# An edge-gated graph layer: PSUM banks of z and of the w_v products filled by VectorE or ScalarE ahead of the matmuls, in fixed banks

## The chip, the cores and the metric

The kernel runs on one core of one Trainium2 chip. The metric is the device time of one execution in microseconds. Times of the kernel before are the median of three runs; the profile is one more execution, taken by the hardware profiler.

## The reference, cut to what matters

There are 16 batches, 1024 nodes, 256 features, and a sparse 1024 x 1024 adjacency `adj` that every batch shares. For each batch:

```python
pre_u = h @ W1[:256];  pre_v = h @ W1[256:]
hidden = relu(pre_u[:, :, None] + pre_v[:, None] + b1)      # per edge u, v
S      = sigmoid(hidden @ W2 + b2)
a_t    = einsum('uv,ud->vd', S * adj, h)
m_t    = einsum('uv,ud->vd', adj, h) * h
z      = beta1*h + beta2*(a_t @ Wa + ba) + beta3*(m_t @ Wm + bm)
```

The change touches how b1 enters `pre_v`, and how `beta1*h` and the biases enter `z`.

## The kernel before, in words

**Blocks and steps.** The output is made in 32 blocks: 4 groups of 4 batches times 8 tiles of 128 target nodes. A block has 10 steps (two windows of 64 targets, five columns of 128 edges each), so there are 320 steps, counted n; k is the block and s the step in it. Groups 0 and 1 come first, interleaved, then group 2 (blocks 16 to 23) and group 3 (24 to 31).

**One step.** POOL gathers, for 128 edges, the rows of their source nodes out of a table in DRAM (`fetch`, L515): the first half of a row holds h times w_u for 4 batches, the second half h itself. TensorE spreads the target's w_v products over the edges with a 0/1 matrix (`expand`, L610, tile `pc`, two buffers). VectorE adds `pc` to the fetched row (`add`, L646, the operation at L648), then takes relu times W2 and its sum once per batch (`gate`, L650, four operations at L656). ScalarE makes the sigmoid (L659) and scales four pieces of the left matrix with it (L661); `left_adj` (L619, L625) prepares the left matrix of the entry after. TensorE then sums the edges into `acc` (`aggregate`, L664, L673), with entries n-3 and n-2 taken at odd steps n.

**Once per half window.** ScalarE copies `acc` to `ev` (`half_end`, L678), TensorE transposes it and ScalarE copies the result into `LT` (`turn_over`, L683, L691 and L694), and VectorE multiplies one half by h (L705).

**Once per block.** `halves` (L473) makes the w_v products of the next block in two parts of two batches: a PSUM bank gets b1 from a matmul of `unit` by a row pair `b1_p` (`add_row`, L448), eight matmul records (L445) add the product, and ScalarE copies the bank twice, to `X` (L482) and `low` (L483); VectorE takes the difference (L484), and ScalarE makes three casts of it, each at a step of its own (L486, L489). `rows` (L452) makes w_u products for the table of a later group and stores them. `block_end` (L710) makes z of the block before, again in two parts: bias row by `add_row`, w_a matmuls in one step, w_m matmuls in the next (L722), ScalarE copies the bank into `LT`'s space (L736), VectorE forms beta1 h + z (L737) a step later, and SP sends the result out (L739). In group 3 the second part adds beta1 h by identity matmuls instead (L726), and ScalarE writes the result (L728).

**PSUM.** `pc` takes four banks (two buffers of two), `acc0` and `acc1` one each, and a pool `psm` of two buffers serves all else in turn (`small`, L220): transposes, w_u, w_v and z products, list products.

**What sets the order.** All five engines run in the order of the program (`manual_schedule`, L492). In the main loop (L882) step n of the program holds, for n below LAST = 230: aggregation and `ev` copies, mark cast (when s is 1 or 6), `expand(n + 2)`, `products(n, k, s)` (L821), `add(n + 1)`, `gate(n)`, `left_adj(n + 1)`, then what is due (`do(n)`, L904). From LAST on, `expand(n + 2)` and `products` stand after `gate`, `left_adj` and `do`. In `products`, z of the block before stands at s = 4, 5, 6, 7, the parts of `halves` at s = 1, 3, 4, 6, 7 (from step 10 on) and transposes at s = 8, 9, 0, 2. `plan` (L787) gives the steps of the loads of hT and of the w_u parts. For the first 110 steps, `lists` (L242) builds the edge lists of later tiles in pieces between VectorE's other work (`fill`, L640).

Of the kernel before, what the change touches and what calls it, by code (L numbers as in the profile page):

```python
# [13 lines left out]
P = 128  # L14
# [3 lines left out]
def kernel(  # L18
# [46 lines left out]
    GB = 4  # L65
# [116 lines left out]
    unit = fixed([P, P], "unit", FR)  # L182
    nc.vector.tensor_scalar(unit, upto[:, :P], 0.0, None, ALU.is_ge)
# [34 lines left out]
    psm = main.enter_context(tc.tile_pool(name="psm", bufs=2, space=bass.MemoryType.PSUM))  # L218

    def small(name):  # L220
        return psm.tile([P, 512], FP, name="misc")
# [20 lines left out]
    def lists(vt):  # L242
# [35 lines left out]
        used = lst.tile([P, S], FP, name="used", bufs=4)  # L278
# [9 lines left out]
        for i in range(4):  # L288
            nc.tensor.matmul(pw[:, i:i + 1], sums[:, i].rearrange("p w q v -> p (w q v)"), R[:, 0:1],
                             start=True, stop=True)  # L290
        yield "wait"
        first = R[:, 1:2]
        from_ = lst.tile([P, 1], FP, name="from", bufs=4)
# [23 lines left out]
        none = lst.tile([P, 1], FP, name="none", bufs=4)  # L317
# [6 lines left out]
        last = lst.tile([P, 1], FP, name="last", bufs=4)  # L324
# [4 lines left out]
        RR = lst.tile([P, NW, RC], FP, name="RR", bufs=2)  # L329
        few = lst.tile([P, E], mybir.dt.uint8, name="few", bufs=2)  # L330
# [13 lines left out]
        L = lst.tile([P, M, RC], FP, name="L", bufs=2)  # L344
# [103 lines left out]
    def add_row(p, parts):  # L448
        nc.tensor.matmul(p, unit, parts.unsqueeze(1).to_broadcast([P, 2, D]),  # L449
                         start=True, stop=False, skip_group_check=True)  # L450
# [22 lines left out]
    def halves(k):  # L473
        X = cuts[k] = big.tile([P, NW, GD], FR, name="X")
        low = one.tile([P, GD], FP, name="low")
        for h in range(2):
            step = yield
            c = slice(2 * h * D, (2 * h + 2) * D)
            p = small("p")
            add_row(p, b1_p)  # L480
            half_product(p, hTs[order[k]], w_v, h, True)
            nc.scalar.copy(X[:, 0, c], p)  # L482
            nc.scalar.copy(low[:, c], p)  # L483
        after(step + (2 if k else 1), lambda: nc.vector.tensor_tensor(low, low, X[:, 0, :].bitcast(FP), ALU.subtract))  # L484
        yield
        nc.scalar.copy(X[W:, 1, :], X[W:, 0, :].bitcast(FP))  # L486
        for w in range(NW):
            yield
            nc.scalar.copy(X[(1 - w) * W:(2 - w) * W, w, :], low[w * W:(w + 1) * W])  # L489
# [16 lines left out]
    T = TW * NW  # L506

    BS = NG * NT
# [28 lines left out]
    b1_b = load_rows(b1, D, "b1_b", nc.sync, spare[:, 0])  # L537
# [92 lines left out]
    be1_eye = []  # L630
# [79 lines left out]
    def block_end(k):  # L710
# [3 lines left out]
        for h in range(2):  # L714
            for i, wt in ((1, w_a), (0, w_m)):
                step = yield
                if i:
                    pz = small("pz")
                    add_row(pz, bias_p)
# [4 lines left out]
            if h == 1 and g == NG - 1:  # L724
                for bb in range(2):
                    nc.tensor.matmul(pz[:, bb * D:(bb + 1) * D], be1_eye[0], hb[h][:, bb, :], start=False, stop=True,  # L726
                                     skip_group_check=True)
                nc.scalar.copy(hb[h], pz.rearrange("p (b d) -> p b d", b=2))  # L728
                b = g * GB + 2 * h
                after(step + 2, lambda hb=hb[h], b=b: nc.sync.dma_start(  # L730
                    out[b:b + 2, vt * P:(vt + 1) * P, :].rearrange("b p d -> p b d"), hb))
                continue
            z = pz.rearrange("p (b d) -> p b d", b=2)
            if step >= ROOM:
                z = LTs[k][:, 2 * h].rearrange("p k c n -> p (k c n)").rearrange("p (b d) -> p b d", b=2)
                nc.scalar.copy(z, pz.rearrange("p (b d) -> p b d", b=2))  # L736
            after(step + 1, lambda hb=hb[h], z=z: nc.vector.scalar_tensor_tensor(hb, hb, be1, z, ALU.mult, ALU.add))  # L737
            b = g * GB + 2 * h
            after(step + 2, lambda hb=hb[h], b=b: nc.sync.dma_start(  # L739
# [53 lines left out]
    plan(turn[NT:], ((1, 2, 4), (2, 8, 9), (5, 12, 18), (10, 19, 22), (20, 28, 29), (23, 32, 38), (30, 39, 42), (40, 48, 49)))  # L793
    for g, first in ((2, 60), (3, 140)):
        plan([(g, vt) for vt in range(NT)], ((first - 4 + 10 * i, first + 8 + 10 * i, first + 12 + 10 * i)
# [25 lines left out]
    def products(n, k, s):  # L821
# [4 lines left out]
        z = 3 if n < ROOM else 4  # L826
        if z <= s < z + 4 and 0 < k < BS:
            if s == z:
                end = block_end(k - 1)
                next(end)  # L830
            go(end, n)
        if ROOM <= n < total - T:
# [18 lines left out]
        later = n >= ROOM  # L851
        if k + 1 < BS and s - later in (0, 2, 3, 5, 6):
            if s == later:
                parts = halves(k + 1)
                next(parts)
            go(parts, n)

# [4 lines left out]
    ROOM, MORE, LISTS = 10, 3, 110  # L862
    LAST = (BS - NT - 1) * T
# [18 lines left out]
    for n in range(total + 2):  # L882
        k, s = divmod(n, T)
# [9 lines left out]
        if n < LAST:  # L893
# [3 lines left out]
            products(n, k, s)  # L897
        if n + 1 < total:
# [10 lines left out]
        if n == 1:  # L909
            bias = load_rows(bm, D, "bias", nc.sync, spare[:, 1])  # L910
# [24 lines left out]
        if n >= LAST:  # L935
            products(n, k, s)
        if n == LISTS:
# [4 lines left out]
            be1_eye.append(more.tile([P, P], FP, name="be1_eye"))  # L942
            nc.vector.tensor_scalar(be1_eye[0], ident, be1, None, ALU.mult)
# [118 lines left out]
```

## Time and profile before

| what | value |
| --- | --- |
| time, median of 3 runs | 1072.59 us (1072.10 to 1073.26) |
| the profiled execution | 1082.24 us |
| its span, mean granted TensorE clock | 1080.4 us, 0.99 |
| DMA | 394.56 MB, mean 365 GB/s |
| chain that ended last, by engine | PE 40%, DVE 34%, issue 10%, ACT 8%, DMA 5% |
| L656, VectorE relu times W2 | 1280 times, mean 419 ns |
| L648, VectorE addition of pc | 320 times, mean 1212 ns |
| L737, VectorE beta1 h + z | 55 times, mean 744 ns |
| L449, TensorE b1 rows and bias rows | 64 and 62 times, mean 411 and 397 ns |
| L726, TensorE identity matmuls | 28 times, mean 379 ns |

PE is TensorE's matmuls, PEld its weight loads, DVE is VectorE, ACT is ScalarE, POOL is GpSimd, SP the engine that issues most transfers. Matmuls overlap in the record, and so do operations of VectorE and ScalarE with the one after: what an operation costs its queue is read as the distance from its start to the next start, which is shorter than its mean.

### The profile page before, as it was taken

How to read it: one execution, taken by the hardware profiler on the slowest of the kernel's cores; microseconds unless marked ns; L12 is line 12 of the kernel's file. 1: busy time of each engine (PE TensorE's matmuls, PEld its weight loads, DVE VectorE, ACT ScalarE, POOL GpSimd, SP SyncE). 2: the span in 40 equal slices, each digit the busy share in tenths (PEclk: the TensorE clock that was granted, in tenths of full speed). 3: DMA queues.
4: the chain of work that ended last, by engine and by line, in shares of the span. 5: the costliest groups of instructions: out<-in, count | busy, mean ns of one | idle time of the engine just before them, and what ended most of it. 6: DMA issues, size and time to landing. Idle time of an engine off the chain costs nothing.

```text
span 1080.4 us, 24120 instructions
## 1 busy us (share of the span) xinstructions
PE 1020.1 (94%) x7673; PEld 731.3 (68%) x7673; DVE 1017.6 (94%) x3481; ACT 862.6 (80%) x2616; POOL 459.3 (43%) x456
## 2 busy tenths in 40 slices
PE   7777999999999999999999999999999999999996
PEld 6654676776666776677777767777766667666654
DVE  8687999998999999999999999999999999999993
ACT  3246787788888887898888888889889889999983
POOL 2666676555257334553333334333333333333330
PEclk9989999999999999999999999999999999999999
DMA  9999899999999999999999999999999999999991
GB/s 283 327 340 385 313 339 381 362 382 378 403 352 371 408 381 385 379 403 395 404 393 399 412 384 392 408 396 389 381 361 370 369 348 368 365 381 369 365 341 44
DMA packets 147752, 394.56 MB, mean 365 GB/s; under 512 B 18224, under 2 KB 94512, under 8 KB 111408
## 3 DMA queue, kind: packets, MB, share of 16 engines
q0 software_dynamic: 50544, 301.16, 70.9%
q1 hardware_dynamic: 83776, 78.66, 22.9%
q10 hardware_dynamic: 13296, 13.11, 3.5%
q8 instruction: 63, 1.03, 0.4%
q14 instruction: 73, 0.60, 0.1%
HBM read 396.93 MB, written 50.33 MB: 414 GB/s over the span
## 4 chain that ended last, share of the span: by engine, by line
PE 40%; DVE 34%; issue 10%; ACT 8%; DMA 5%; POOL 2%; another core or an unknown queue 0%; POOLq 0%; DVEq 0%; ACTq 0%
DVE fetched L656 16%; DVE fetched L648 12%; PE acc L673 10%; PE misc L722 10%; PE misc L445 9%; PE pc L615 7%; DMA fetched<-table,uidx 3%; PE misc L691 2%; ACT left L661 2%; DVE LT L705 1%; ACT X L489 1%; PE misc L449 1%; DVE low L484 1%; DVE h_blk L737 1%; DMA hT__635<-in_xT_dram 1%
## 5 line engine op out<-in xcount | busy, mean ns | idle before, releaser
L518 POOL DMA_INDIRECT fetched<-table,uidx x320 | 339.4, 1061 | 529.0 <-PE acc L673 389.0
L656 DVE SCALAR_TENSOR_TENSOR fetched<-fetched,w_b 128x256 f32<-128x256 f32 x1280 | 478.0, 419 | 0.0
L648 DVE TENSOR_TENSOR fetched<-fetched,pc 128x1024 f32<-128x1024 f32 x320 | 387.7, 1212 | 29.9 <-PE pc L615 19.4
L661 ACT ACTIVATE left<-left,gt 128x32 f32<-128x32 f32 (+1 forms) x1280 | 299.6, 305 | 10.4
L673 PE MATMUL acc<-fetched,left 128*32 128x256 f32 x4096 | 273.4, 385 | 6.3 <-ACT gt L659 3.7
L615 PE MATMUL pc<-X,mark 128*128 128x512 f32 x640 | 243.7, 462 | 10.9 <-DVE fetched L648 9.3
L673 PEld LDWEIGHTS acc<-fetched,left 128*32 128x32 f32 x4096 | 127.6, 109 | 112.1 <-issue 29.1
L615 PEld LDWEIGHTS pc<-X,mark 128*128 128x128 f32 x640 | 105.4, 189 | 88.9 <-issue 41.6
L659 ACT ACTIVATE gt<-sc,b_b 128x4 f32<-128x4 f32 x320 | 95.9, 300 | 46.7 <-DVE fetched L656 37.5
L722 PE MATMUL misc<-w_m,LT 128*128 128x256 f32 x496 | 117.3, 379 | 0.0
L722 PE MATMUL misc<-w_a,LT 128*128 128x256 f32 x496 | 117.2, 379 | 0.0
L445 PE MATMUL misc<-w_v,hT 128*128 128x256 f32 x448 | 107.6, 383 | 0.0
L722 PEld LDWEIGHTS misc<-w_a,LT 128*128 128x128 f32 x496 | 93.8, 189 | 15.3 <-issue 0.4
L722 PEld LDWEIGHTS misc<-w_m,LT 128*128 128x128 f32 x496 | 93.8, 190 | 15.1
L625 ACT ACTIVATE left<-onehot,val 128x64 f32<-128x64 bf16 (+1 forms) x320 | 102.9, 322 | 0.0
L385 POOL DMA_INDIRECT val<-in_adjT_dram,vidx x80 | 87.2, 1090 | 34.4 <-issue 20.4
L656 DVE DVE_READ_ACCUMULATOR fetched<-fetched,w_b 128x1 f32 x1280 | 100.7, 79 | 0.0
L691 PE MATMUL misc<-ident,ev 128*128 128x128 f32 x512 | 79.5, 278 | 18.5 <-issue 7.0
L445 PEld LDWEIGHTS misc<-w_v,hT 128*128 128x128 f32 x448 | 86.4, 193 | 14.3
L691 PEld LDWEIGHTS misc<-ident,ev 128*128 128x128 f32 x512 | 60.7, 141 | 45.7 <-ACT ev L681 15.2
L482 ACT CAST X<-misc 128x512 fp32r<-128x512 f32 x64 | 37.1, 580 | 55.2 <-PE misc L445 48.0
L445 PE MATMUL misc<-w_u,hT 128*128 128x256 f32 x320 | 76.6, 386 | 4.0 <-issue 3.8
(185 smaller groups left out, 1011.3 us busy)
## 6 DMA issues: line engine op xcount, KB each, us to landing
h_blk<-table SPq DMA_DIRECT2D x62, 256.0 KB
out_dram<-h_blk SPq DMA_DIRECT2D x62, 256.0 KB
hT<-in_xT_dram SPq DMA_DIRECT2D x28, 512.0 KB
table<-in_x_dram ACTq DMA_DIRECT2D x24, 512.0 KB
table<-tab SPq DMA_DIRECT2D x48, 256.0 KB
fetched<-table,uidx POOLq DMA_INDIRECT x320
table<-in_x_dram SPq DMA_DIRECT2D x8, 512.0 KB
table<-fetched SPq DMA_DIRECT2D x8, 512.0 KB
```

The costliest lines, as they stand in the source:

```text
L385: nc.gpsimd.indirect_dma_start(out=val[:, i, j:j + 1], out_offset=None, in_=adj_flat, in_offset=bass.IndirectOffsetOnAxis(ap=vidx[:, i, j: ...
L445: nc.tensor.matmul(p[:, bb * D:(bb + 1) * D], hT[:, 2 * h + bb, i, :], wt[:, i, :], start=(i == 0 and not begun), stop=(i == DC - 1), skip ...
L518: nc.gpsimd.indirect_dma_start(out=fetched[at_slot[n]], out_offset=None, in_=table[g], in_offset=bass.IndirectOffsetOnAxis(ap=uidx[:, vt * ...
L615: nc.tensor.matmul(pcs[n][:, c], marks[n // TW][:, j * P:(j + 1) * P], cuts[k][:, w, c], start=True, stop=True)
L625: nc.scalar.activation(lefts[n][:, :m, 1::GB, :], onehot[:, i, o:o + m, :].unsqueeze(2).to_broadcast([P, m, GB // 2, V]), AF.Copy, scale=v ...
L648: nc.vector.tensor_tensor(t, t, pcs.pop(n), ALU.add)
L656: nc.vector.scalar_tensor_tensor(t[:, b, :], t[:, b, :], 0.0, w2_b, ALU.max, ALU.mult, accum_out=sc[:, b:b + 1])
L659: nc.scalar.activation(gt, sc, AF.Sigmoid, bias=b2_b)
L661: nc.scalar.activation(lefts[n][:, :m, 2 * b, :], lefts[n][:, :m, 1 + b // 2 * GB, :], AF.Copy, scale=gt[:, b:b + 1])
L673: nc.tensor.matmul(accs[h][b * 2 * V:(b + 1) * 2 * V, r, :], left[:, i, 2 * b - b % 2:2 * b - b % 2 + 2].rearrange("p k v -> p (k v)"), f[ ...
L691: nc.tensor.transpose(pt[:, r, :, c, :], ev[:, r, c * P:(c + 1) * P], ident)
L722: nc.tensor.matmul(pz[:, bb * D:(bb + 1) * D], LTs[k][:, 2 * h + bb, i if bb else 1 - i, c, :], wt[:, c, :], start=False, stop=(i == 0 and ...
```

## The change

Bank 1 of `psm` becomes the bank of z and of the w_v products, bank 0 that of everything else (from step 10 to three steps before the end). The additive part is written into bank 1 ahead of the matmuls, which then all add. `seed_x` copies b1 into it by ScalarE (steps 11 to 221, at s = 9 and s = 1). `seed_z` writes beta1 h + bias by VectorE before step 230, or beta1 h by ScalarE from then on, where the bias row stays as an adding matmul; it stands at s = 3 and s = 6 (s = 5 for the last block). The identity matmuls, the VectorE operation after z and the copy into `LT` are gone; ScalarE copies z's bank to `h_blk`, and the transfer out follows a step later. The w_v parts stand a step sooner, the second part of z a step later, the w_u parts at other steps.

```diff
+    unit_ = fixed([P, 1], "unit", FR)
+    nc.vector.tensor_scalar(unit_, row, 0.0, None, ALU.is_ge)
+    unit = unit_.to_broadcast([P, P])
...
-    psm = main.enter_context(tc.tile_pool(name="psm", bufs=2, space=bass.MemoryType.PSUM))
-    def small(name):
-        return psm.tile([P, 512], FP, name="misc")
+    psm = main.enter_context(tc.tile_pool(name="psm", bufs=1, space=bass.MemoryType.PSUM))
+    def small(name, bank=None):
+        if bank is None and ROOM <= now[0] < BS * T - 3:
+            bank = 0
+        elif bank is None:
+            bank = turn_of[0] % 2
+            turn_of[0] += 1
+        return psm.tile([P, 512], FP, name=f"misc{bank}")
...
+        if vt >= EARLY - 1:
+            held_pw = lst.tile([P, 4], FP, name="pws", bufs=2)
+            nc.scalar.copy(held_pw, pw[:, :4])
+            pw = held_pw
...
+    def seed_x():
+        p = small("p", 1)
+        nc.scalar.copy(p.rearrange("p (b d) -> p b d", d=D), b1_b.unsqueeze(1).to_broadcast([P, 2, D]))
+        seeds.append((p, False))
+
+    def seed_z(k, h, step):
+        p = small("pz", 1)
+        out_ = p.rearrange("p (b d) -> p b d", d=D)
+        if step < LAST:
+            nc.vector.scalar_tensor_tensor(out_, hbs[k][h], be1, bias.unsqueeze(1).to_broadcast([P, 2, D]), ALU.mult, ALU.add)
+        else:
+            nc.scalar.activation(out_, hbs[k][h], AF.Copy, scale=be1)
+        seeds.append((p, step >= LAST))
...
-            p = small("p")
-            add_row(p, b1_p)
+            if seeds:
+                p = seeds.pop()[0]
+            else:
+                p = small("p", 1 if step >= ROOM else None)
+                add_row(p, b1_p)
...
                 if i:
-                    pz = small("pz")
-                    add_row(pz, bias_p)
+                    pz, bare = seeds.pop()
+                    if bare:
+                        add_row(pz, bias_p, False)
...
-                    nc.tensor.matmul(pz[:, bb * D:(bb + 1) * D], be1_eye[0], hb[h][:, bb, :], start=False, stop=True,
...
-                nc.scalar.copy(z, pz.rearrange("p (b d) -> p b d", b=2))
-            after(step + 1, lambda hb=hb[h], z=z: nc.vector.scalar_tensor_tensor(hb, hb, be1, z, ALU.mult, ALU.add))
+            nc.scalar.copy(hb[h], pz.rearrange("p (b d) -> p b d", b=2))
             b = g * GB + 2 * h
-            after(step + 2, lambda hb=hb[h], b=b: nc.sync.dma_start(
+            after(step + 1, lambda hb=hb[h], b=b: nc.sync.dma_start(
...
-    plan(turn[NT:], ((1, 2, 4), (2, 8, 9), (5, 12, 18), (10, 19, 22), (20, 28, 29), (23, 32, 38), (30, 39, 42), (40, 48, 49)))
+    plan(turn[NT:], ((1, 2, 4), (2, 8, 9), (5, 11, 13), (10, 16, 21), (14, 23, 26), (22, 31, 33), (27, 36, 41), (34, 43, 46)))
-        plan([(g, vt) for vt in range(NT)], ((first - 4 + 10 * i, first + 8 + 10 * i, first + 12 + 10 * i)
+        plan([(g, vt) for vt in range(NT)], ((first - 4 + 10 * i, first + 6 + 10 * i, first + 13 + 10 * i)
...
-        z = 3 if n < ROOM else 4
-        if z <= s < z + 4 and 0 < k < BS:
-            if s == z:
+        zs = (4, 5, 6, 7) if k == BS - 1 else (4, 5, 7, 8)
+        if s == zs[2] - 1 and s == 6 and 0 < k < BS:
+            seed_z(k - 1, 1, n)
+        if s in zs and 0 < k < BS:
+            if s == zs[0]:
...
+        if s == 5 and k == BS - 1:
+            seed_z(k - 1, 1, n)
...
-        later = n >= ROOM
-        if k + 1 < BS and s - later in (0, 2, 3, 5, 6):
-            if s == later:
+        if k + 1 < BS and s in (0, 2, 3, 5, 6):
+            if s == 0:
...
+    def seed(n, k, s):
+        if ROOM < n < LAST and (s == 9 and k + 2 < BS or s == 1 and k + 1 < BS) and n + 1 < LAST:
+            seed_x()
+        if s == 3 and 0 < k < BS:
+            seed_z(k - 1, 0, n)
...
             products(n, k, s)
+            seed(n, k, s)
```

Left out: seven list tiles have fewer buffers, b1 and the bias rows get tiles of their own instead of a borrowed one, and `be1_eye` with its one VectorE operation is dropped. `seed` follows `products` in both branches of the main loop.

## The prediction

> **What bounds the kernel now.** I read the page's busy line first, then the engines' windows, then who waits for whom in two stretches, then the timeline of one block. The page:
>
> ```profile
> PE 1020.1 (94%) x7673; PEld 731.3 (68%) x7673; DVE 1017.6 (94%) x3481; ACT 862.6 (80%) x2616; POOL 459.3 (43%) x456
> ```
>
> TensorE and VectorE tie, so averages decide nothing. The timeline's VectorE additions (L648), every tenth, give the length of each ten-step block: 31 to 37 us for blocks 1 to 6 and 9 to 11 (those with lists, mostly), 30.0 to 30.3 for blocks 7, 8 and 12 to 22 (31.3 for block 17), 28.9 for blocks 23 and 24, 28.2 for 25 to 30. The windows of the two clean stages (columns: length, then PE, PEld, DVE, ACT, POOL):
>
> ```profile
> 475.00:778.00 303.00, 301.15 (x2325) 219.10 (x2323) 290.73 (x954) 263.86 (x812) 107.61 (x102) 1.00 1.02 397
> 865.00:1034.00 169.00, 165.86 (x1320) 117.98 (x1320) 169.00 (x565) 152.94 (x473) 60.97 (x60) 1.00 0.96 363
> ```
>
> In the middle TensorE is full, in the last stage VectorE is, with TensorE at 98% and ScalarE at 90%. The waits agree. Middle stage:
>
> ```profile
> DVE fetched L648 <- PE pc L615: 13.2, 14, 1.2
> ```
>
> Last stage, all the waits of TensorE's matmuls, six blocks together:
>
> ```profile
> PE misc L691 <- ACT ev L681: 2.5, 4, 0.7
> PE misc L691 <- ACT LT L694: 1.2, 2, 0.6
> ```
>
> So TensorE waits only 0.6 us a block there: 28.2 - 0.6 = 27.6 us of its own work. The change puts new waits on exactly this engine. One block's steps 3 to 5 in the last stage, timeline:
>
> ```profile
> 929.59 1.20 DVE L648 TENSOR_TENSOR fetched<-fetched,pc 128x1024 f32<-128x1024 f32 x1
> ...
> 931.67 0.81 PE L615 MATMUL pc<-X,mark 128*128 128x512 f32 x2
> ...
> 932.21 0.30 ACT L659 ACTIVATE gt<-sc,b_b 128x4 f32<-128x4 f32 x1 [0.52 <-DVE fetched L656]
> 932.32 0.39 PE L449 MATMUL misc<-bias_p,unit 128*128 128x512 f32 x1
> 932.54 0.96 ACT L661 ACTIVATE left<-left,gt 128x32 f32<-128x32 f32 x4
> 932.55 1.89 PE L722 MATMUL misc<-w_a,LT 128*128 128x256 f32 x8
> ...
> 933.40 0.30 ACT L625 ACTIVATE left<-onehot,val 128x32 f32<-128x32 bf16 x1
> ...
> 936.23 0.73 PE L615 MATMUL pc<-X,mark 128*128 128x512 f32 x2
> ...
> 936.78 1.04 ACT L486 CAST X<-X 64x1024 fp32r<-64x1024 f32 x1
> 936.80 1.89 PE L722 MATMUL misc<-w_m,LT 128*128 128x256 f32 x8
> ...
> 938.90 1.21 DVE L648 TENSOR_TENSOR fetched<-fetched,pc 128x1024 f32<-128x1024 f32 x1
> ```
>
> The addition at 929.59 is that of entry 4 (step 3). TensorE starts step 4's w_a (bias row at 932.32) while ScalarE is only at step 3's gate (932.21): TensorE runs a step ahead of ScalarE.
>
> **What the Trainium skill says.** PSUM — Partial Sum Buffer, Engine vs sequencer instructions: ScalarE and VectorE queues are strict FIFO, and matmuls start in program order. The trace agrees: gate, left and the next left at 932.21, 932.54 and 933.40 stand as written. The same page, The four PSUM rules: VectorE and ScalarE writes leave the has-written bits alone, and a matmul without the start flag adds where an earlier one set the bit; bank 1 gets full rows with start first, so the sums should hold. No run here shows it yet. Perfetto Trace Analysis, Matmuls: independent groups should rotate through banks, so that evacuation overlaps the next group. Before, two rotate, and the middle stage shows next to no matmul wait on an evacuation. Prices: ScalarE: Activation LUTs, What ACT_TABLE_LOAD costs, has 186 ns + 0.833 per element, 93 more for a pointer scale, 93 overlapped: estimates of 0.52 us start to start for an x seed of 512 and 0.61 for a z seed with be1. For the 32-wide pointer form the page gives 0.307, the trace 0.310.
>
> **The change, part by part** (durations start to start in the timeline, which is what a queue pays).
>
> Rows off TensorE. A row costs 0.23 (932.32 to 932.55). x seeds run at steps 11 to 221: 43 b1 rows gone; z seeds before step 230: 44 bias rows gone. In blocks 2 to 22 that is 4 x 0.23 = 0.9 us a block. The 28 identity matmuls (L726) took 0.67 a block of 25 to 31.
>
> VectorE. 55 scaled additions (L737, 0.66 each) become 44 fills, the same operation with PSUM as output. Nothing in the trace shows that output; Perfetto Trace Analysis, Optimizing Scalar/DVE Operations, has 60 ns overhead on SBUF and 125 on PSUM, so 0.66 to 0.73 and below 0.66 only if the write were faster; I take 0.66. Eleven fall away: 0.66 a block in 25 to 31, 1.3 in 23 and 24.
>
> ScalarE. The 62 evictions of z stay. Added: 43 x seeds and 18 z seeds, about 1.1 us a block: 26.8 to 27.9 of work in the middle, 26.1 to 27.2 in the last stage.
>
> Moves. The w_v products go to steps 0 and 2, the rest of their casts and low with them; w_u to steps 3 and 6; the second z to 7 and 8. SP's out transfers follow the eviction instead of VectorE, h_blk must be there 24 us after its issue instead of 33, hT loads have one to six steps less before use (their pieces of w_u come up to six steps sooner). POOL's gathers keep their place behind the aggregations and come later only if those do. No time to landing is printed; at the 363 to 397 GB/s of the windows 256 KB is 0.7 us, and VectorE waited for fetches only 2.7 us in all. I take 0, up to 2 us in the first blocks. List buffers cut to one and five small copies of pw: 0 to 1 us, within slack; I take 0.
>
> **New wait, last stage, first z.** The seed is ScalarE's last act of step 3; behind it on TensorE's queue stand w_a, the aggregation and the next pc, for which VectorE waits. w_v's two evictions, 0.96, now stand ahead of gate 3, which had waited 0.52 idle; with what lies before, gate 3 starts some 0.36 later, 932.57. Then gate 0.33, left 0.86, next left 0.24, the X cast that moved to step 3 1.05, seed 0.61, 0.1 to signal: 935.8. Before, the row began at 932.32, so 3.5 late. From there to the second pc is 3.91 (932.32 to 936.23), and an addition follows a pc by 0.85: 935.8 + 3.9 + 0.85 = 940.5, against 938.90. TensorE, with w_v done earlier, would now stand idle some 3.1 us. From both sides: w_v's end to seed is at least 4.2 (0.96 + 0.33 + 0.86 + 0.24 + 1.05 + 0.61 + 0.15), TensorE has 1.44 + 0.57 + 0.6 = 2.6 to do: 1.6 at least, 3.5 at most.
>
> **Second z.** From w_m's last matmul: its end 0.35, eviction 0.48, X cast 1.05, mark 0.62, gate 0.33, left 0.86, next left 0.24, seed 0.61, signal 0.1 = 4.6; TensorE meanwhile has pc 0.65, aggregation 1.0, pc 0.57 = 2.2: idle 2.4. TensorE's block is then 27.6 - 0.67 + 3.1 + 2.4 = 32.4, less w_v's shorter edges, say 32.0, above VectorE's 28.2 - 0.7 = 27.5: +3.8 a block. Blocks 23 to 30, the first counted half: 7.5 x 3.8 = +28 (with the least wait 30.9, +20; with the most +32).
>
> **Middle stage.** ScalarE seeds w_v's second half in step 1, after step 0's gate. From w_v's first matmul: eviction starts 1.93 later (606.00 to 607.93), X 0.49, low 0.47, gate 0.34, left 0.87, next left 0.24, ev 0.47, mark 0.62, seed 0.52, signal 0.1 = 6.05. TensorE: w_v 1.82, aggregation 1.44, two pc 1.17, transposes 0.5 = 4.93. Idle 1.1, which eats the 0.9. In bank 0 the transposes of steps 8, 9 and 0 follow one another, each behind its predecessor's copy, 0.3 each for two. 30.1 - 0.9 + 1.1 + 0.6 = 30.9; I take +0.6, as an early copy may save part: 13 blocks, +8 (0 to +12). VectorE's fills wait for the same evictions, inside its 1 us of spare per block and TensorE's waits.
>
> **List stage.** VectorE was 98% busy; TensorE's saving is cover only, and a fill reaches its place about when the eviction ends (6.35 against 6.6 us after entry 2's addition, by the same sums). 0, from -3 to +4. **End**: block 31 has no w_v, so the waits find room: -0.5.
>
> Sum: 8 + 28 - 0.5 = +35.5 on a span of 1080.4; the profiled execution took 1082.24 (1.8 outside the span), the median is 1072.59, 0.991 of it: +35, so 1108. Its own range is 1090 to 1121 (0 + 20 - 3 and 12 + 32 + 4).
>
> **Rivals.**
> 1. Faster: seeds come in time. TensorE may idle 28.2 - 26.9 = 1.3 us per block in the last stage before anything is lost; if ScalarE keeps the two waits under that together, VectorE's 27.5 holds there (-6.6 over eight blocks) and TensorE's 29.2 in the middle (-0.9 x 13 = -12): 1054. For it: ScalarE is at 90%. Against: the order of its queue, not its load, makes the seeds late.
> 2. Only the last stage loses: the middle saves its 0.9 (the x seed does not bind), -12 + 28 = +16: 1089. For it: TensorE ran late there, with VectorE waiting on it.
> 3. Cancelled: least waits shared with other idle time, +12 late, -12 in the middle: 1073. If the bits were not set, rows would be lost, and the time would be as forecast.
>
> **How the numbers follow.** Forecast 0.54, rival 1 0.20, rival 2 0.20, rival 3 0.06. About 0.2%, 2 us, can be told from no change. Faster: rival 1 and a third of 3, 0.22; same 0.04; slower 0.74. The range takes in half of rival 1: 1058 to 1121, with 0.10 left below and 0.05 above.
>
> **What would show it.** Right: in the last stage TensorE waits 4 to 6 us a block, named ScalarE's seed line before w_a, blocks near 32 us, VectorE waiting for pc; in the middle about 1 us before w_v at step 2, blocks 30 to 31. Wrong: w_a starting within 0.5 us of the pc before it in blocks 25 to 30, or middle blocks of 29.2.

## The result, and the profile after

| | before | after |
| --- | --- | --- |
| median of 4 runs | 1072.70 us | 1174.39 us (1173.83 to 1174.84) |
| profiled execution's span | 1080.4 us | 1172.0 us |
| mean granted TensorE clock | 0.99 | 0.961 |

The ratio is 1.0948, 95% interval 1.0929 to 1.0967: slower by 102 us, where 35 were forecast, and outside the range. The profile before was of a long execution (9.5 us over its median), the one after of a median one, so the spans differ by 91.6 only; the other 10 us have no place in the two traces. In profiles with the code of before (itself, e12, e17, e19) blocks of the last stage repeat within 0.2 us, while the way to step 111 varies by 7 us, so the ten probably lie there. If so, the start and the list stage lost more than is counted here.

Step by step (start of ScalarE's mark cast, after against before): by step 1 the changed kernel is 4.4 us ahead, by step 111 it is 14.3 behind, by step 231 28.9, by step 301 80.6, at the end 91.6. So the list stage lost 18.6 us (forecast 0), the middle 14.6 (forecast 8), the last stage and the end 62.7 (forecast 27.5): 57.5 up to step 311 (forecast 28), and 5.3 behind it (forecast -0.5). The start is no effect: over all the profiles below it lies between 4.5 us earlier and 3.3 later.

The page's busy line: each engine is busy for less of the span than before.

```profile
PE 1039.8 (89%) x7558; PEld 719.5 (61%) x7558; DVE 1012.5 (86%) x3469; ACT 899.9 (77%) x2682; POOL 461.5 (39%) x456
```

The windows of a middle and of a last stretch (length, PE, PEld, DVE, ACT, POOL, clock, DMA share, GB/s):

```profile
495.00:798.00 303.00, 291.07 (x2185) 203.43 (x2183) 278.42 (x914) 263.71 (x792) 100.02 (x97) 1.00 1.00 383
877.00:1055.00 178.00, 145.96 (x1082) 98.38 (x1081) 139.37 (x465) 134.77 (x406) 53.05 (x51) 0.93 0.84 290
```

In the last stretch no engine is full any more, and one column differs that the prediction left aside: the clock, 0.93 where it had been 1.00. TensorE's waits in five blocks of the last stage:

```profile
PE misc L466 <- ACT misc L482: 29.0, 10, 3.4
PE misc L723 <- ACT LT L726: 3.0, 5, 0.6
```

L466 is the bias row, L482 ScalarE's z fill: two waits a block. One block's first fill, timeline of TensorE and ScalarE:

```profile
1024.33 1.20 PE L648 MATMUL pc<-X,mark 128*128 128x512 f32 x4
...
1025.16 0.58 ACT L519 COPY low<-misc 128x512 f32<-128x512 f32 x1
1025.64 0.30 ACT L691 ACTIVATE gt<-sc,b_b 128x4 f32<-128x4 f32 x1
1025.97 0.96 ACT L693 ACTIVATE left<-left,gt 128x32 f32<-128x32 f32 x4
...
1027.15 1.04 ACT L522 CAST X<-X 64x1024 fp32r<-64x1024 f32 x1
1028.21 0.69 ACT L482 ACTIVATE misc<-h_blk,be 128x512 f32<-128x512 f32 x1
...
1028.96 0.49 PE L466 MATMUL misc<-bias_p,unit 128*128 128x512 f32 x1 [3.43 <-ACT misc L482]
...
1029.29 3.25 PE L755 MATMUL misc<-w_a,LT 128*128 128x256 f32 x8
```

The bank is free at about 1025.7, when low is copied; the fill starts 2.5 us later, behind gate, left and a cast. That is the order that the prediction followed. What it didn't foresee stands in the last line: eight w_a matmuls take 3.25 us instead of 1.89. The windows around them say why (the clock is the third column from the end):

```profile
1028.90:1031.00 2.10, 2.04 (x6) 1.68 (x7) 2.10 (x5) 1.42 (x7) 0.00 (x0) 0.68 0.84 226
1031.00:1033.00 2.00, 2.00 (x12) 0.97 (x14) 1.02 (x6) 0.00 (x0) 0.00 (x0) 0.50 0.90 377
1033.00:1036.00 3.00, 3.00 (x38) 1.93 (x31) 0.63 (x1) 1.92 (x7) 1.57 (x2) 0.99 0.33 63
```

What these clocks fall short of 1 makes 1.7 us in the three windows together: TensorE is granted half its clock for 3.4 us. All eight first waits of blocks 23 to 30 (3.3 to 3.4 us) are followed by slow w_a matmuls; of the eight second ones (2.37 us) three are, from block 24 on every other one (w_a then takes 3.0 to 3.2 us, else 1.9), and blocks alternate between 35.0 and 36.5 us. The Trainium skill, TensorE: Matmul & The Clock Gate, What's actually happening, has this: the clock is half or full, drops after an idle window of some 3.4 us, comes back after as much work, and the window runs freely, so where a wait falls in it counts. The trace agrees, but for the size: here 2.37 us of idle time is enough when it falls badly, and two shorter waits close together can be (e2 below).

Behind step 311 the last block's fills are late as well, and its w_a is slow:

```profile
1133.49 0.79 PE L466 MATMUL misc<-bias_p,unit 128*128 128x512 f32 x1 [2.76 <-ACT misc L482]
1134.08 3.62 PE L755 MATMUL misc<-w_a,LT 128*128 128x256 f32 x8
```

In e1, without ScalarE's z fills, this end is 1.0 us longer than before instead of 5.3.

In the middle stage TensorE's waits are small, and before there was one of 1.2 us in four blocks, yet blocks take 31.43 us instead of 30.15. Four blocks:

```profile
PE misc L462 <- ACT misc L473: 1.8, 4, 0.5
PE misc L723 <- ACT ev L713: 1.8, 4, 0.4
PE misc L723 <- ACT LT L726: 0.8, 4, 0.2
```

That is 0.45 us at w_v (L462) for ScalarE's b1 fill, 0.45 at transposes (L723) for `ev`, 0.2 at transposes for the copy of their predecessor. In the list stage (steps 1 to 111) VectorE, the fullest engine there before, stands at its z fill (L480) for ScalarE's copy of low:

```profile
DVE misc L480 <- ACT low L519: 17.5, 9, 4.7
```

The clock falls there, too. Block by block, the windows' clocks fall short of 1 by 12.0 us in all, before by 3.4. At half clock that is 24 and 7 us, and TensorE has up to 8.5 us more to make up: an estimate, and an upper bound, as e13's list stage falls short by 13.8 and is only 4.9 us longer than before.

### The profile page after: what moved, and what is told of

It is laid out like the page before. It is cut to its first block, busy times and chain, and to the rows that moved or that the text cites. A ratio compares the mean times of both kernels' runs of the same rounds, so it can differ in the third digit from the quotient of the medians.

```text
span 1172.0 us, 23990 instructions
## 1 busy us (share of the span) xinstructions
PE 1039.8 (89%) x7558; PEld 719.5 (61%) x7558; DVE 1012.5 (86%) x3469; ACT 899.9 (77%) x2682; POOL 461.5 (39%) x456
## 4 chain that ended last, share of the span: by engine, by line
PE 57%; ACT 21%; DVE 12%; DMA 5%; issue 3%; ACTq 0%; SPq 0%; DVEq 0%
PE misc L462 16%; PE misc L755 15%; PE acc L705 13%; PE pc L648 7%; ACT left L693 5%; DVE fetched L688 5%; PE misc L723 4%; DVE fetched L680 3%; DMA table<-tab 3%; ACT LT L726 2%; DMA hT<-in_xT_dram 2%; ACT mark L583 2%; ACT X L518 2%; ACT gt L691 1%; ACT low L519 1%
## 5 line engine op out<-in xcount | busy, mean ns | idle before, releaser
L648 PE MATMUL pc<-X,mark 128*128 128x512 f32 x640 | 233.8, 456 | 17.8 <-DVE fetched L680 15.4
L705 PEld LDWEIGHTS acc<-fetched,left 128*32 128x32 f32 x4096 | 130.0, 110 | 122.7 <-issue 38.1
L755 PE MATMUL misc<-w_a,LT 128*128 128x256 f32 x496 | 133.9, 419 | 0.0
L462 PE MATMUL misc<-w_v,hT 128*128 128x256 f32 x448 | 112.2, 394 | 9.5 <-ACT misc L473 8.3
L755 PEld LDWEIGHTS misc<-w_a,LT 128*128 128x128 f32 x496 | 104.8, 211 | 18.6
L723 PE MATMUL misc<-ident,ev 128*128 128x128 f32 x512 | 82.0, 283 | 25.7 <-ACT LT L726 14.4
L713 ACT COPY ev<-acc 128x512 f32<-128x512 f32 x128 | 73.2, 572 | 39.0 <-PE acc L705 38.5
L462 PEld LDWEIGHTS misc<-w_v,hT 128*128 128x128 f32 x448 | 83.6, 193 | 25.2 <-ACT misc L473 12.1
L723 PEld LDWEIGHTS misc<-ident,ev 128*128 128x128 f32 x512 | 58.6, 142 | 64.3 <-ACT LT L726 36.1
L726 ACT COPY LT<-misc 128x512 f32<-128x512 f32 x128 | 73.0, 570 | 9.8 <-PE misc L723 9.8
```

Source lines behind the costliest of these rows:

```text
L462: nc.tensor.matmul(p[:, bb * D:(bb + 1) * D], hT[:, 2 * h + bb, i, :], wt[:, i, :], start=(i == 0 and not begun), stop=(i == DC - 1), skip ...
L648: nc.tensor.matmul(pcs[n][:, c], marks[n // TW][:, j * P:(j + 1) * P], cuts[k][:, w, c], start=True, stop=True)
L705: nc.tensor.matmul(accs[h][b * 2 * V:(b + 1) * 2 * V, r, :], left[:, i, 2 * b - b % 2:2 * b - b % 2 + 2].rearrange("p k v -> p (k v)"), f[ ...
L723: nc.tensor.transpose(pt[:, r, :, c, :], ev[:, r, c * P:(c + 1) * P], ident)
L726: nc.scalar.copy(LT.rearrange("p b k c (r v) -> p r (b k c) v", v=V)[:, r:r + 2], pt.rearrange("p r k c v -> p r (k c) v"))
L755: nc.tensor.matmul(pz[:, bb * D:(bb + 1) * D], LTs[k][:, 2 * h + bb, i if bb else 1 - i, c, :], wt[:, c, :], start=False, stop=(i == 0 and ...
```

## The experiments

The comparison is by typical lengths of blocks in the profiles, which agree from chip to chip within 0.1 us in the middle and last stages where the code and the clock are the same, and by ratios to the kernel before on the same chip; its own median was 1072 to 1088 there. Gains in us below are differences of medians; on the chip of e1, e2, e4 and e5 the kernel before took 4 us more than on the changed kernel's, so by the ratios they are larger: 58, 51, 12 and 25. In the traces, step 231 to the end has 53, 46 and 21 us less in e1, e2 and e5. The list stage's excess (steps 1 to 111 over those of the profile before) is less firm: five kernels with the changed kernel's code there have 17.8 to 21.9 us, four with the code of before (itself, e12, e17 and e19) -0.7 to 6.9.

| kernel | list excess | middle block | last block | ratio (95%) |
| --- | --- | --- | --- | --- |
| before | 0 | 30.15 | 28.2 | 1 |
| after | 18.6 | 31.43 | 35.8 | 1.0948 (1.0929 to 1.0967) |
| e1 rows in the last stage | 21.9 | 31.4 | 29.65 | 1.0404 (1.0356 to 1.0452) |
| e2 last fills early | 17.8 | 31.4 | 30.4 | 1.0469 (1.0420 to 1.0517) |
| e4 z fills late | 7.9 | 31.4 | 35.9 | 1.0834 (1.0782 to 1.0886) |
| e5 TensorE kept busy | 19.5 | 31.4 | 33.4 | 1.0713 (1.0651 to 1.0774) |
| e3 b1 fills early | 20.7 | 31.9 | 35.9 | 1.0917 (1.0863 to 1.0971) |
| e6 no fills | 12.6 | 31.25 | 29.65 | 1.0412 (1.0350 to 1.0473) |
| e7 all three moves | 7.1 | 31.9 | 30.4 | 1.0428 (1.0360 to 1.0497) |
| e8 rows, banks in turn at the end | 20.3 | 31.4 | 29.2 | 1.0369 (1.0314 to 1.0423) |
| e9 no fills, banks in turn | 14.7 | 30.85 | 29.3 | 1.0266 (1.0219 to 1.0312) |
| e11 z fills moved | 23.8 | 31.4 | 30.4 | 1.0478 (1.0438 to 1.0517) |
| e14 e9, w_u back | 8.6 | 33.85 | 29.3 | 1.0578 (1.0534 to 1.0622) |
| e16 e9, w_u and w_v exchanged | 16.1 | 29.8 | 29.3 | 1.0259 (1.0213 to 1.0304) |

**e1, rows in the last stage.**

```diff
     def seed_z(k, h, step):
+        if step >= LAST:
+            return
...
-                    if bare:
-                        add_row(pz, bias_p, False)
+                    if step >= LAST:
+                        pz = small("pz", 1)
+                        add_row(pz, bias_p)
...
+            if step >= LAST:
+                for bb in range(2):
+                    nc.tensor.matmul(pz[:, bb * D:(bb + 1) * D], be1_eye[0], hb[h][:, bb, :], start=False, stop=True,
```

> Undoes ScalarE's z fills from step 230 on alone: there the bias row opens bank 1 again and the matmul by beta1 times the identity adds h, as before the change; fixed banks, the moved schedule and all fills up to step 229 stay. Theory A (the last stage's 62.7 us are TensorE's waits for the two z fills of a block, 3.43 and 2.37 us, and what the clock loses after them): the waits at the bias row go, blocks fall from 35.75 to 28 or 29 us, the time by 52 to 63 us to 1111 to 1122. Rival B (the single bank 1 and the schedule cost the last stage its time, whoever fills the bank): blocks stay over 32 us, the time over 1145.

Blocks of 29.65, 53 us less: theory A holds for all but 1.45 us a block, which stays of the 7.6 lost. Not all is as before here: both parts of z now get beta1 h by identity matmuls, before only the second. e6, where only the second does, has the same 29.65.

**e2, last fills early.**

```diff
-        if s == 3 and 0 < k < BS:
+        if s == (2 if n >= LAST else 3) and 0 < k < BS:
             seed_z(k - 1, 0, n)
...
-        if s == 5 and k == BS - 1:
+        if s == 5 and n >= LAST and 0 < k < BS:
             seed_z(k - 1, 1, n)
```

> Moves ScalarE's z fills in its queue alone, from step 230 on: each stands right behind the eviction that frees bank 1 (the first in step 2 behind the last w_v eviction, the second in step 5 behind the eviction of the first z), instead of behind the gates of the next steps. Same fills, same banks, same load. Theory A (order: the fill is ready late because ScalarE's gate work stands ahead of it): the waits of 3.43 and 2.37 us nearly go, blocks 27.5 to 29 us, the time 1108 to 1122. Rival B (load or the single bank: eviction, fill and product of one bank can only follow each other): TensorE still waits 2 us or more for each fill, blocks over 32 us, the time over 1145.

The time is 47 us less, 1127: theory A, though 5 us over its bracket, and the blocks, 30.4, are 1.4 over theirs. Waits of four last blocks in e2:

```profile
PE misc L723 <- ACT LT L726: 8.1, 8, 1.2
PE misc L466 <- ACT misc L482: 3.9, 4, 1.0
```

One fill still comes 1 us late, the other in time; transposes now wait for ScalarE's copies, 2 us a block (0.6 before the move). So the same fills, with the same load on ScalarE, cost 5.4 us a block, wait and clock together, by their place in its queue alone.

One of the eight blocks takes 32.0 us. Its transposes wait 0.86 and 1.17 us within 3.2 us, as in the other seven, but here the clock falls to 0.51 for 3.4 us behind them, and w_v takes 2.9 us instead of 1.9:

```profile
985.55 0.66 PE L723 MATMUL misc<-ident,ev 128*128 128x128 f32 x4 [0.86 <-ACT LT L726]
...
987.84 1.11 PE L723 MATMUL misc<-ident,ev 128*128 128x128 f32 x4 [1.17 <-ACT LT L726]
...
989.18 2.92 PE L462 MATMUL misc<-w_v,hT 128*128 128x256 f32 x8
```

e7 has this once in eight blocks, e11 in none.

**e5, TensorE kept busy.**

```diff
                     if bare:
+                        warm_ = small("warm")
+                        for _ in range(8 if h else 12):
+                            nc.tensor.matmul(warm_, unit, bias_p.unsqueeze(1).to_broadcast([P, 2, D]), start=True, stop=True)
                         add_row(pz, bias_p, False)
```

> Adds matmuls that nobody reads (12 ahead of the first bias row of a block, 8 ahead of the second, in bank 0, which holds nothing at that point) from step 230 on, so that TensorE is busy while it would wait for the z fill; fills, banks and order stay. The fill comes no earlier; only the idle time is filled. Theory A2 (half of the extra over the forecast 32.0 us a block is the clock, which is granted at half for some 4 us after such a wait): the w_a batches behind the waits take 1.9 us each again instead of 3.05 to 3.6, blocks fall from 35.75 to 32 to 33.5 us, the time by 15 to 28 us to 1146 to 1159. Rival E (the slow batches come from something else, such as bank 1 being read while it is written): no batch gets faster, the time stays within 3 us of 1174 or rises by the matmuls' own time.

21 us less, for added work: theory A2. The fill comes no earlier, a rest of the wait is left, and w_a runs at full speed (timeline of e5; L754 are the added matmuls):

```profile
1013.63 2.94 PE L754 MATMUL misc<-bias_p,unit 128*128 128x512 f32 x12
1017.24 0.50 PE L466 MATMUL misc<-bias_p,unit 128*128 128x512 f32 x1 [0.67 <-ACT misc L482]
1017.57 1.89 PE L758 MATMUL misc<-w_a,LT 128*128 128x256 f32 x8
```

The window of 908 to 1042 us has a clock of 1.00. So the lost clock is 35.8 - 33.4 = 2.4 us a block. The three stretches of 3.4 us at half clock in every two blocks of the changed kernel make 2.6 at most, which fits.

**e4, VectorE's z fills late.**

```diff
         do(n)
+        if n < LAST and s in (3, 6) and 0 < k < BS:
+            seed_z(k - 1, s // 6, n)
...
-        if s == 3 and 0 < k < BS:
+        if s == 3 and 0 < k < BS and n >= LAST:
             seed_z(k - 1, 0, n)
```

> Moves VectorE's z fills behind its gate work in steps 3 and 6, up to step 229, so that what frees bank 1 (ScalarE's copy of low, the eviction of the first z) has landed when VectorE comes to the fill; the last stage stays. Theory C (the 18.6 us of steps 1 to 111 come from VectorE standing in its queue for ScalarE's copy of low, 4.7 us at the longest): that wait nearly goes, the early stage gains 10 to 18 us, the middle stage between a gain of 10 and a loss of 5 since TensorE may now wait at w_a; the time 1146 to 1164. Rival D (the early stage loses its time to the fills' own 0.75 us on VectorE, to the single bank or to list pieces that wait for the copied counts): the time within 4 us of 1174.

The wait for low is gone in the list stage, and the time is 9 us less, a microsecond short of theory C's bracket and far from D. e11 below, with the same fills, lost 23.8 us there on another chip, so that gain of the whole isn't firm. The middle block is unchanged: VectorE, which stood there for low as well (10.1 us in four blocks), then waits for pc instead (6.9 us); TensorE bounds that stage.

**e3, b1 fills early.**

```diff
-        if ROOM < n < LAST and (s == 9 and k + 2 < BS or s == 1 and k + 1 < BS) and n + 1 < LAST:
+        if ROOM < n < LAST and (s == 8 and k + 2 < BS or s == 0 and k + 1 < BS) and n + 2 < LAST:
             seed_x()
```

> Moves ScalarE's b1 fills (middle and list stage) one step up in its queue, right behind the two evictions that free bank 1 (steps 8 and 0 instead of 9 and 1). Theory M1 (TensorE bounds the middle stage, and its waits at w_v for the fill, 0.45 us seen and some 0.2 hidden a block, are part of it): they go, a middle block takes 30.7 to 31.0 us instead of 31.43, the time falls by 5 to 12 us to 1162 to 1169. Rival M2 (the saved wait turns up at the transposes that wait for ScalarE's ev, since the fill now stands ahead of ev): the middle block stays within 0.15 us of 31.43, the time within 3 us of 1174.

Neither length comes out; rival M2's cause does, and more strongly than it said. The wait for the b1 fill goes, but blocks grow to 31.9: the fill now stands ahead of `ev` and `LT` on ScalarE, and the transposes wait more than w_v had. Waits of four middle blocks in e3, to be set beside 1.8 and 0.8 above:

```profile
PE misc L723 <- ACT ev L713: 4.4, 4, 1.1
PE misc L723 <- ACT LT L726: 3.6, 8, 0.7
```

**e6, no fills.** `block_end` behind its matmuls is that of before, too.

```diff
     def seed_x():
+        return
...
     def seed_z(k, h, step):
+        return
...
-                    pz, bare = seeds.pop()
-                    if bare:
-                        add_row(pz, bias_p, False)
+                    pz = small("pz", 1 if step >= ROOM else None)
+                    add_row(pz, bias_p)
```

> Takes all fills away: bias and b1 rows by TensorE open every bank again, beta1 h is added as before the change; what stays of the change are the fixed banks and the moved schedule. Theory B0 (fixed banks cost by themselves: the transposes of three steps follow each other in bank 0, each behind its predecessor's copy, and list products hold bank 0 until ScalarE has copied them): the list stage keeps 3 to 8 us, middle blocks 30.7 to 31.3 us against 30.12, last blocks 29.0 to 29.7 against 28.2; time 1087 to 1100. Rival S (all the loss comes with the fills): within 5 us of the kernel before, 1073 to 1078.

1119, more than B0's 1100, and S is far off: without any fill four tenths of the loss remain. The list stage keeps 12.6 us instead of 3 to 8. The first two blocks of the last stage take 31.4 and 32.7 us in this kernel, and about as long in e9 and e16; the cause wasn't sought. In the middle stage the fills make nearly no difference (31.43 against 31.25): what the rows save is spent on the waits.

**e8, rows and banks in turn from step 230.** On top of e1:

```diff
-        if bank is None and ROOM <= now[0] < BS * T - 3:
+        if now[0] >= LAST:
+            bank = None
+        if bank is None and ROOM <= now[0] < LAST:
             bank = 0
```

> The kernel whose last stage has TensorE's rows again, and there two banks in turn instead of the fixed ones, from step 230 on. It lost 1.45 us a block against the kernel before (29.65 against 28.2), with waits of transposes for the copy of their predecessor (3.6 us in four blocks). Theory B1 (these waits come from the single bank 0): last blocks 28.2 to 28.5 us, the time 9 to 12 us under the kernel with the rows alone, 1108 to 1113. Rival S1 (the moved schedule, not the banks): blocks stay at 29.4 to 29.8 us, the time within 3 us of 1121.

Blocks of 29.2: between the two. Of the 1.45 us, 0.45 is the single bank; the other 1.0 is put down to the moved schedule, and e9 below, with the identity matmuls of before, has 29.3.

**e9, no fills and banks in turn.** On top of e6:

```diff
-        if bank is None and ROOM <= now[0] < BS * T - 3:
-            bank = 0
-        elif bank is None:
-            bank = turn_of[0] % 2
-            turn_of[0] += 1
+        bank = turn_of[0] % 2
+        turn_of[0] += 1
```

> The kernel without any fill, now with two banks in turn everywhere as before the change; what is left of the change is the moved schedule (w_v in steps 0 and 2, w_u in other steps, the second z in 7 and 8) with the smaller list buffers. With fixed banks it took 1119. Theory B0' (most of that comes from the banks: the transposes of steps 9, 0 and the w_v behind them queue for bank 0): middle blocks return from 31.2 to 30.1 to 30.4 us, last blocks from 29.7 to 29.2, the list stage gains 4 to 9 us, the time 1086 to 1101. Rival S2 (the moved schedule by itself costs it, whatever the banks): middle blocks stay at 30.9 us or more, the time over 1108.

Middle blocks stay at 30.85, last ones at 29.3: nearer to rival S2 in the blocks. The time decides nothing: 1112 to 1125 us where the kernel before takes 1088, and by the ratio 1101 on the first chip. The fixed banks cost 0.4 us a block there, the moved schedule 0.7. Its timeline shows where (step 2 of a middle block; `issue` in the bracket, though ScalarE's copy of `acc` is what these transposes read):

```profile
716.08 1.19 PE L647 MATMUL pc<-X,mark 128*128 128x512 f32 x4
717.72 0.66 PE L723 MATMUL misc<-ident,ev 128*128 128x128 f32 x4 [0.45 <-issue]
```

Before the change 1.7 us of w_u stood between the two:

```profile
662.29 0.81 PE L615 MATMUL pc<-X,mark 128*128 128x512 f32 x2
662.94 1.89 PE L445 MATMUL misc<-w_u,hT 128*128 128x256 f32 x8
664.66 0.60 PE L691 MATMUL misc<-ident,ev 128*128 128x128 f32 x4
```

`plan` moved it to step 3, and nothing covers the wait now.

**e14 and e16, the cover put back.** In e14, e9's `plan` line gets the numbers of before (8 and 12), which puts w_u in steps 8 and 2. e16, on top of e9:

```diff
-        plan([(g, vt) for vt in range(NT)], ((first - 4 + 10 * i, first + 6 + 10 * i, first + 13 + 10 * i)
+        plan([(g, vt) for vt in range(NT)], ((first - 4 + 10 * i, first + 6 + 10 * i, first + 12 + 10 * i)
...
-        if k + 1 < BS and s in (0, 2, 3, 5, 6):
+        if k + 1 < BS and s in ((0, 3, 4, 6, 7) if 70 <= n < 230 else (0, 2, 3, 5, 6)):
```

> The kernel without fills, with two banks in turn and the moved schedule, but in the middle stage w_u's pieces back in steps 8 and 2, where one stands ahead of the transposes of step 2 again. Theory C2 (the lost cover of these transposes is what the moved schedule costs the middle stage): TensorE's wait of 0.45 us there goes, middle blocks fall from 30.9 to 30.1 to 30.5 us. Rival W (w_v's new places cost it: its row and products follow the transposes at once, in both steps): blocks stay at 30.7 to 31.0 us. Last blocks, which have no w_u, stay at 29.2 to 29.4 either way.

> The kernel without fills, with two banks in turn and the moved schedule; from step 70 to 229 w_v's second half goes to step 3 and w_u's piece to step 2, ahead of the transposes there. Theory C2 (the lost cover of the transposes of step 2 costs the middle stage its 0.75 us a block): no wait of 0.45 us at these transposes, middle blocks 30.1 to 30.5 us instead of 30.9. Rival W (w_v's first half in step 0, right behind transposes, or the second z in steps 7 and 8 costs it): middle blocks stay at 30.7 to 31.0 us.

e14 told nothing of its question: w_u and w_v met in step 2 and blocks took 33.85 us. e16 answers it: blocks of 29.8, 1.0 less, where the wait had been 0.45. Theory C2, with the whole of the 0.7 back and 0.3 more; as the exchange also takes w_v's second half away from those transposes, the share of the cover alone isn't separated. The two lines from e16:

```profile
678.58 1.89 PE L459 MATMUL misc<-w_u,hT 128*128 128x256 f32 x8
680.30 0.60 PE L723 MATMUL misc<-ident,ev 128*128 128x128 f32 x4
```

Fixed banks would hardly allow this exchange: with w_v's second half in step 3, its evictions, the fill and w_a of step 4 would follow each other in bank 1; it wasn't tried there.

**e7 and e11, the moves together**: e2, e3 and e4 at once, and without e3.

> All three moves of fills at once: ScalarE's z fills and its b1 fills right behind the eviction that frees bank 1, VectorE's z fills behind its gate work. If the gains of the single moves add up (47 us in the last stage, 12 in the list stage, and what the early b1 fill gives by itself), the time is 1104 to 1116. Rival: the moves hamper each other on ScalarE, whose gates for VectorE then come later, and the time stays over 1118. Either way it stays above the kernel before, since the fixed banks remain.

> The changed kernel with both moves of z fills that gained (ScalarE's right behind the evictions in the last stage, VectorE's behind its gate work before), the b1 fills left where they are. If the two gains (47 and 12 us) add: 1111 to 1118, middle blocks 31.4 as in the changed kernel. If ScalarE's b1 fills are not what made middle blocks 31.9 with all three moves, but VectorE's late z fills are, the middle blocks stay at 31.9 and the time is 1119 to 1124.

Last blocks of 30.4 in both, and middle ones of 31.9 with the early b1 fills, 31.4 without: e3's loss is the b1 fills' own. The sum of the gains isn't reached. e7 takes 1120 us, over its bracket as its rival said, with the middle blocks of e3. e11 is no better than e2 alone (1.0478), because of its list stage. Its long blocks there have a clock of 0.91 to 0.96, as those of the changed kernel do.

**e12, e13, e17, e18 and e19, early z fills in the old schedule.** The kernel before, with one change: in steps 120 to 229 VectorE fills z's bank at the end of steps 3 and 5.

```diff
+        if LISTS + 10 <= n < LAST and s in (3, 5):
+            pz = small("pz")
+            nc.vector.scalar_tensor_tensor(pz.rearrange("p (b d) -> p b d", d=D), hbs[k - 1][s // 5], be1,
+                                           bias_row.unsqueeze(1).to_broadcast([P, 2, D]), ALU.mult, ALU.add)
+            fills.append(pz)
```

> The kernel before with the one piece of the change that no run speaks against: in steps 120 to 229 VectorE fills the banks of z with beta1 h and bias, at the end of steps 3 and 5, a step ahead of w_a, in its old schedule and with two banks in turn; ScalarE then evicts the finished z, and VectorE's old addition goes. TensorE, which bounds the middle stage, loses two rows of 0.23 us a block, VectorE's work stays (0.67 for 0.67). Theory T (a fill that is a step early costs nothing): blocks of 30.12 take 29.6 to 29.8 us, the time falls by 3 to 6 us, ratio 0.994 to 0.997. Rival V (VectorE had 1.2 us to spare a block and the fill makes TensorE or its own queue wait): ratio 0.998 to 1.005.

> Once more the kernel before, in its old schedule and with two banks, with VectorE's z fills a step early in steps 120 to 229. The second w_v half now takes the bank of the transposes ahead of it, so that a fill stands in a bank that TensorE last wrote over its whole width, and w_u's product opens its bank once instead of once per half. Theory T (as measured by blocks of 29.7 against 30.15 us in the version before this): blocks of 29.7 us, 3 to 6 us less, ratio 0.994 to 0.998. Rival V2 (w_v's second half now waits for the copy of the transposes ahead of it in its bank): blocks of 30.1 us or more, ratio 0.999 to 1.004.

> The kernel before with VectorE's early z fills in steps 120 to 229 (not in step 153), each in a bank that TensorE last wrote over its whole width: w_v's second half takes the bank of the transposes ahead of it, w_u's product opens its bank once from step 110 on, and nothing differs before step 110. Theory T (TensorE loses two rows of 0.23 us in each of 11 middle blocks, nothing else waits): middle blocks 29.7 us, 4 to 5 us less, ratio 0.995 to 0.998. Rival V4 (the gain doesn't reach the end, or drowns in the spread of the list stage): ratio 0.999 to 1.004.

> As the run before (the kernel before with VectorE's early z fills in steps 120 to 229 but 153, in banks that TensorE last wrote over their whole width), with the pool of two banks of the kernel before up to step 110 and the banks in strict turn only from there on. Theory T: list stage as before, middle blocks 29.7 us against 30.15, ratio 0.995 to 0.998. Rival V5 (the gain is too small beside the spread of the list stage or is lost at the change of pools): ratio 0.998 to 1.002.

In e12 z isn't whole (relative error 0.34). A reason that fits stands in the Trainium skill, PSUM — Partial Sum Buffer, The four PSUM rules: a matmul with the start flag clears the bits of its whole bank. So of four transposes only the last would leave its columns set, and where a fill lies in a bank that they wrote last, a later sum would overwrite the rest of beta1 h and bias. e13, e18 and e19 put the fill into a bank last written over its whole width, and z is whole. e17 was to do so by leaving out one turn of the pool, and its z isn't whole either (relative error 0.32); the trace doesn't name the bank that its fills lay in. The ratios are, in the order of the runs, 0.9985 (0.9963 to 1.0007), 1.0040 (1.0021 to 1.0060), 0.9994 (0.9972 to 1.0016), 1.0070 (1.0048 to 1.0091) and 1.0003 (0.9986 to 1.0020). Middle blocks are 29.7 us in all five: two rows of 0.23 saved, as theory T has it. It doesn't reach the whole. In e12, e13, e18 and e19 one fill waited 1.4 to 4.4 us for its h. In e13 and e18 the banks were taken in strict turn from the start, and in e18's list stage products (L448) and transposes (L696) waited 11.5 us for VectorE to read counts out of a bank (its excess there is 12.7 us, e13's 4.9):

```profile
PE misc L448 <- DVE from L303: 7.2, 2, 4.4
...
PE misc L696 <- DVE from L303: 4.3, 1, 4.3
```

No version here beats the kernel before.

## Why the prediction was wrong, step by step

**Right: the waits of the last stage.** First z forecast 3.1 us, seen 3.43; second 2.4, seen 2.37; the cause, fills behind other work in ScalarE's queue, confirmed by e2. What they cost at full clock was right, too: 3.8 us a block forecast, 3.75 shown (e5 less e1).

**Failed: what a wait costs.** The step "TensorE's block is then 27.6 - 0.67 + 3.1 + 2.4" added idle time to durations at full clock, in an otherwise unchanged block. Two terms were missing: 2.4 us of half clock (e5), and 1.45 from the moves, 0.45 of it for bank 0 and 1.0 put down to the schedule (e1, e8). 28.2 + 1.45 + 3.75 + 2.4 = 35.8, the block that was seen. By blocks, 7.5 x 7.6 = 57 instead of 28.

**Failed: the end at -0.5.** "block 31 has no w_v, so the waits find room" took its two waits to be covered. They were 2.76 and 0.94 us, with slow w_a matmuls behind the first, and the end took 5.3 us more.

**Failed: "Moves ... I take 0".** They were searched for late transfers and late uses, but not for cover that goes away with them. Late transfers weren't it: after the change 256 KB of `h_blk` took 8.9 us to land, far over the estimate of 0.7, and yet TensorE waited for transfers only 1.6 us more in all (5.7 before, 6.2 and 1.1 after). w_u left step 2, and the transposes there had nothing ahead of them. The moved schedule costs 0.7 us a middle block (e9 against before), and putting w_u back ahead of them, in exchange with w_v, more than makes up for it (e16). With this 0.7, the middle's +0.6 a block becomes +1.3. Of its other terms the fixed banks were near (forecast 0.6, shown 0.4, e6 less e9). The fills' net, +0.2, came out as forecast (after less e6), but by luck in part: the wait before w_v, taken as 1.1, shows as 0.45, and where the rest of the 0.9 went wasn't followed up.

**Failed: the list stage at 0.** "a fill reaches its place about when the eviction ends" rested on a margin of 0.25 us, worked out with durations of other stages; ScalarE was later, by up to 4.7 us, and VectorE had little slack there. e4 shows that this wait can go. How much of the 18.6 us it makes stays open: without fills 8.6 to 16.1 us of the excess remain (e6, e9, e14, e16), with late ones 7.1 to 7.9 (e4, e7) and once 23.8 (e11). Which of the fills, the moves, the smaller list buffers and the clock makes how much wasn't separated. The traces show products waiting up to 2.7 us for copies of list products (L306), and clocks of 0.91 to 0.96 in the longest blocks.

**The rivals.** All three put the outcome below the forecast. The first, fills in time, came nearest to being tried in e2 and e7: with fills about 1 us late at most, the time is still 4% over before. What the moves cost stays, and so do waits of transposes of 2 us a block. The range's upper end was the forecast's own with the longest waits. That a wait lowers the clock was stated on a page that the prediction didn't draw on, and the windows of the profile have a column for it.

ScalarE's fill itself took 0.72 us start to start (1028.21 to 1028.93) against an estimate of 0.61; that is 0.2 us a block.

## What to carry to other kernels

A wait of TensorE can have two prices: its length, and matmuls at half clock after it, here another 40% of the two waits (2.4 on 5.8 us); find such gaps in the windows' clock column, and fill them if they can't be removed. Work that another engine does ahead for a matmul belongs right behind what frees its place, and must then be checked for what it delays in its own queue (e2 gained, e3 lost). When a schedule is moved, ask of each product not only when it is needed, but which wait it was covering where it stood.

## What the runs showed of the hardware that was not expected

A wait of 2.37 us halved the clock in three blocks of eight, one of 3.3 to 3.4 us in each, for 3.4 us at a time. In e2, two waits of 0.86 and 1.17 us shortly after each other did so in one block of eight, so no single length decides. Matmuls that nobody reads, 12 and 8 of a row each, made the changed kernel 21 us faster (1174 to 1153).
